# First-layer window attention: scores and weights turned and spread through DRAM by DMA, in place of transposes and spreading matmuls on TensorE

## The chip, the core and the metric

The kernel runs on one core of one Trainium2 chip. The metric is the device time of one execution in microseconds; the median of the runs shown is given. Engines are called PE (TensorE, matmul), DVE (VectorE), ACT (ScalarE), POOL (GpSimd) and SP (SyncE, which here only issues transfers).

## The reference, cut to what matters

The program is four layers, each an attention with a residual and a feed-forward part with a residual, on x of 16 x 64 x 512 values with a context of the same shape, all in 32-bit floats. The change touches only the attention of layer 0, a window attention. Its 64 rows are channels (8 heads of 8), its 512 columns are positions, and each position looks at 16 neighbours:

```python
q = _pointwise(Wq, bq, layernorm(x))        # 64x64 weights, over channels
k = _pointwise(Wk, bk, cond); v = _pointwise(Wv, bv, cond)
k = jnp.pad(k, ((0, 0), (0, 0), (8, 7))); v = jnp.pad(v, ((0, 0), (0, 0), (8, 7)))
idx = jnp.arange(T)[:, None] + jnp.arange(16)[None, :]
dots = jnp.einsum('bhdt,bhdtw->bhtw', qh, k_win) * 8 ** -0.5
attn = softmax(dots, axis=-1)               # over the 16 offsets w
out = jnp.einsum('bhtw,bhdtw->bhdt', attn, v_win)
return _pointwise(Wo, bo, out)
```

After it come an int8-like feed-forward part (layer 0), a grouped attention with normed queries and keys (layer 1), an MXFP4 feed-forward part, and layers 2 and 3.

## The kernel before

**Tiles.** The tokens lie in 8 tiles of 128 rows (two batch entries of 64) by 512 columns. The first layers work on four pairs of tiles.

**Two lanes and the order of TensorE.** Lane a (`main`) runs layer 1's attention, `normed_attention`; lane b (`side`) runs ahead of it through layer 0 (`first_layers`: `WindowAttention`, then `Int8Ffn`), pair by pair. Both are generators that yield a cost in ticks after each step. `merged` draws them together: for each tick of `main` it advances `side` by `rate` ticks, and a `Need` makes it advance `side` until a mark is passed. This order is TensorE's program order (`manual_schedule` for PE alone). The other engines and the SP queue are ordered by a scheduler from expected readiness and this order. While lane b does the first pair, lane a computes its context keys (`context_keys`, L679, rate 1.1). After that, lane a's heads run over one pair (16 units of 11.4 ticks) while lane b prepares the next pairs, at the rates of the list in `main`: 0.88, 0.8, 0.8, 0.72 for the four pairs.

**Window attention on one pair** (`weights`, then `output` for each tile). A tile's 128 rows are 16 heads of 8 channels, so a pair has NH = 32 heads. For each of 4 groups of 4 offsets, DVE multiplies queries by shifted keys into `prod` (L293), and PE sums each head's 8 channels with a 0/1 matrix into a bank whose 128 rows are 4 offsets by 32 heads (L300). ACT copies it to `dots` (L308). A softmax over the offsets needs them along a row, so PE transposes `dots` by quarters of 128 positions (`ps_dotT`, L316); DVE takes maximum, difference and sum (L324, L325, L328), ACT the exponential (L326), POOL the scaling (L330); PE turns the result back (`ps_att`, L137 through `transposed`), and ACT copies it to `att` (L338).

`output` must give each of a tile's 128 channels the weight of its head. For each group of offsets, PE multiplies 32 rows of `att` by a 0/1 matrix `spread` for each of 4 offsets (`ps_exp`, L367); DVE multiplies by the shifted values into `pv` (L377); POOL adds the upper two products to the lower two (L379), then the remaining two into `acc` (L383, or L385 and L386). `project` multiplies `acc` by the output weights on PE (L356). `n_sums` says how many `acc` are projected per tile: 4 for the first pair (one per group), 1 for the others. DVE adds bias and residual (L395).

**Buffers.** `prod` and `pv` share 2 buffers of 4 x 512 values per row; `e` and the context tiles share 3 of 512; lane b has 4 of the 8 PSUM banks.

**Transfers.** All are issued from SP's queue, in order. In this part they are lane a's: weights (L622, 1.5 MB, and L631, 1 MB, each once for two units), saved context keys and values (`s`, L701; loads L714 and L719). Lane b has only the context tiles (L247).

Of the kernel before, what the change touches and what calls it, by code (L numbers as in the profile page):

```python
# [46 lines left out]
PAGE = 2048  # L47

# [149 lines left out]
class WindowAttention:  # L198
# [6 lines left out]
    def __init__(self, es, ln, ctx_in, wt, bias):  # L205
# [7 lines left out]

        self.spread = pool.tile([P, 2 * P], F32, tag="spread", name="spread")
# [7 lines left out]
        for w in range(self.NG):  # L222
            rows = slice(w * NH, (w + 1) * NH)
            nc.vector.tensor_copy(
                self.spread[rows].rearrange("p (h d) -> p h d", d=8),
                bc(k.ident[rows, rows], 2, 8),
            )
# [17 lines left out]
    def context(self, t):  # L245
        cn = self.pool.tile([P, D], F32, tag="row", name="cn", bufs=3)
        self.ln.nc.sync.dma_start(cn, self.ctx_in[t * P : (t + 1) * P, :])  # L247
        return cn
# [23 lines left out]
    def products(self, name):  # L272
        return self.pool.tile([P, self.NG, D], F32, tag="prod", name=name, bufs=2)

    def weights(self, tiles):
# [8 lines left out]
        for xn, cn in zip(xns, cns):  # L284
            self.kept.append(self.inputs(xn, cn))
            yield 3.0
        dots = pool.tile([P, WIN // NG, D], F32, tag="dots", name="dots")
        for g in range(WIN // NG):
# [19 lines left out]
            nc.scalar.copy(dots[:, g, :], ps)  # L308

        self.att = pool.tile([P, WIN // NG, D], F32, tag="att", name="att")  # L310
        es_of = {}
        for c in range(NC + 2):
            if c < NC:
                ps = ln.bank([P, WIN, NH], "ps_dotT")
                for g in range(WIN // NG):
                    nc.tensor.transpose(  # L316
                        ps[:, g * NG : (g + 1) * NG, :].rearrange("p w h -> p (w h)"),
                        dots[:, g, c * P : (c + 1) * P],
                        ln.k.ident,
                    )  # L320
                e = pool.tile([P, D], F32, tag="row", name="e", bufs=3)
                e = e.rearrange("p (w h) -> p w h", w=WIN)
                mx = ln.small.tile([P, NH], F32, tag="mx0", name="mx0")
                nc.vector.tensor_reduce(mx, ps.rearrange("p w h -> p h w"), AX.X, ALU.max)  # L324
                nc.vector.tensor_tensor(e, ps, bc(mx, 1, WIN), ALU.subtract)  # L325
                nc.scalar.activation(e, e, AF.Exp, scale=8.0**-0.5)  # L326
# [5 lines left out]
            if c <= NC:  # L332
                yield 3.0
# [1244 lines left out]
```

## Time and profile before

| | |
|---|---|
| median of three runs | 1778.39 us (1776.37 to 1782.56) |
| profiled execution, its own time | 1772.04 us |
| its span, first to last instruction | 1770.2 us |
| busy: PE, DVE, ACT, POOL | 1686.6, 965.3, 615.3, 501.4 us |
| mean granted clock of PE | 0.991 |
| DMA | 154.23 MB, 25.7% of 16 engines' span on the main queue |
| layer 0 attention | from 8 to 819 us, beside lane a's work |
| lane a's first query matmul | 213.5 us |

A row of the profile's groups gives line, engine, operation, what is written and read, the count, the busy time and the mean of one in ns, and after it the idle time of that engine just before these instructions and what ended it. A 32-bit matmul leaves two records, so "x256" of `ps_exp` are 128 matmuls. A line of the timeline gives start, duration, engine, line, operation and the number of merged records, and in brackets the idle time before it. Waits of the SP queue are given as total, number and longest, in us.

### The profile page before, as it was taken

What the parts mean: (1) busy time and instruction counts of PE and PEld (TensorE: products, weight loads), DVE (VectorE), ACT (ScalarE), POOL (GpSimd) and SP (SyncE); (2) the same over time, 40 slices, a digit from 0 to 9 for tenths busy, and PEclk for the clock granted to TensorE, in tenths of its full rate; (3) what the DMA queues carried; (4) which work ended last, traced back from release to release, by engine and by line L of the source; (5) the groups of instructions that cost most, each with busy time, mean ns of one, the idle gap of its engine ahead of it and who ended that gap; (6) DMA issues with size and microseconds to landing.
All of it is one profiled execution on the core that took longest, in us unless ns stands there. A gap on an engine that the chain in (4) does not pass through costs nothing.

```text
span 1770.2 us, 21537 instructions
## 1 busy us (share of the span) xinstructions
PE 1686.6 (95%) x7592; PEld 960.9 (54%) x7596; DVE 965.3 (55%) x2042; ACT 615.3 (35%) x1933; POOL 501.4 (28%) x494
## 2 busy tenths in 40 slices
PE   7999999999999999999999999999999999999999
PEld 2323455565554665555655656655566655556664
DVE  6644477666665656556587426648425534521335
ACT  2312244334432434424334335521224422223332
POOL 1443225632245431366222213310112201110012
PEclk9989999999999999999999999999999999999999
DMA  9211223213232333222263233031211011111120
GB/s 295 94 66 60 90 79 104 93 66 127 83 128 69 105 105 104 92 105 92 72 238 118 79 106 139 27 116 48 87 43 66 19 45 48 42 66 44 36 66 24
DMA packets 62362, 154.23 MB, mean 87 GB/s; under 512 B 31536, under 2 KB 40624, under 8 KB 50352
## 3 DMA queue, kind: packets, MB, share of 16 engines
q1 hardware_dynamic: 62256, 152.86, 25.7%
q8 instruction: 61, 1.00, 0.2%
q14 instruction: 45, 0.37, 0.1%
HBM read 142.35 MB, written 10.49 MB: 86 GB/s over the span
## 4 chain that ended last, share of the span: by engine, by line
PE 46%; DVE 6%; POOL 3%; ACT 3%; DMA 1%; issue 1%; SPq 0%; ACTq 0%; POOLq 0%; DVEq 0%
PE ps_wo L592 9%; PE ps_q L1291 4%; PE ps_q L722 3%; PE ps_o L1144 3%; PE ps_h L1119 3%; PE ps_a L583 3%; PE ps_s L543 2%; PE ps_v L1238 2%; PE ps_k L1275 2%; PE ps_pT L137 2%; PE ps_kv L740 2%; PE ps_wo L1035 2%; PE ps_q L967 2%; PE ps_o L1206 2%; ACT p L558 1%; PE ps_v L946 1%
## 5 line engine op out<-in xcount | busy, mean ns | idle before, releaser
L592 PE MATMUL ps_wo<-l1a_o,aT 128*128 128x512 f32 x512 | 234.4, 601 | 0.8 <-issue 0.6
L722 PE MATMUL ps_q<-l1a_w,kvT 128*128 128x512 f32 x512 | 230.8, 593 | 0.0
L567 POOL TENSOR_TENSOR p<-p,sm 128x512 f32<-128x512 f32 x96 | 105.9, 1103 | 437.4 <-DVE sm L566 380.5
L558 ACT ACTIVATE p<-ps_s,mx 128x128 f32<-128x128 f32 x384 | 135.5, 367 | 247.6 <-DVE mx L554 210.8
L119 POOL TENSOR_TENSOR r<-r,mhalf 128x5 f32<-128x5 f32 (+1 forms) x96 | 101.9, 1062 | 284.2 <-DVE r L669 279.9
L592 PEld LDWEIGHTS ps_wo<-l1a_o,aT 128*128 128x128 f32 x512 | 95.5, 192 | 121.0 <-issue 120.0
L722 PEld LDWEIGHTS ps_q<-l1a_w,kvT 128*128 128x128 f32 x512 | 92.7, 190 | 96.7 <-issue 96.6
L141 DVE TENSOR_TENSOR x<-x,ps_wo 128x512 f32<-128x512 f32 x104 | 70.6, 679 | 132.8 <-PE ps_wo L592 106.9
L740 PE MATMUL ps_kv<-l1a_w,kvT 128*128 128x256 f32 x512 | 124.2, 386 | 5.0 <-ACT qn L732 2.6
L679 PE MATMUL ps_ckv<-l1a_kv,kvT 128*64 128x512 f32 x512 | 123.2, 625 | 2.3 <-DMA l1a_kv<-in_l1a_kv 2.3
L668 DVE TENSOR_REDUCE r<-sq 128x5 f32<-128x640 f32 (+1 forms) x96 | 65.4, 682 | 108.4 <-ACT sq L748 55.6
L740 PEld LDWEIGHTS ps_kv<-l1a_w,kvT 128*128 128x128 f32 x512 | 93.4, 192 | 20.2 <-ACT qn L732 4.3
L119 POOL TENSOR_TENSOR rs<-rs,mhalf 128x1 f32<-128x1 f32 x64 | 37.1, 583 | 220.0 <-DVE rs L128 213.3
L553 DVE TENSOR_REDUCE mx<-ps_s 128x4 f32<-128x512 f32 x96 | 65.6, 684 | 61.2 <-PE ps_s L543 61.2
L756 DVE TENSOR_TENSOR qn<-qn,r 128x512 f32<-128x512 f32 x64 | 47.6, 743 | 92.3 <-POOL r L119 91.1
L543 PEld LDWEIGHTS ps_s<-kT,qT 128*128 128x128 f32 (+1 forms) x704 | 89.1, 192 | 14.7 <-issue 5.5
L379 POOL TENSOR_TENSOR pv<-pv 128x1024 f32<-128x1024 f32 x32 | 75.2, 2350 | 71.9 <-DVE pv L377 66.5
L543 PE MATMUL ps_s<-kT,qT 128*128 128x128 f32 (+1 forms) x704 | 92.1, 277 | 0.0
L137 PE MATMUL ps_pT<-ident,p 128*128 128x128 f32 x512 | 75.3, 276 | 16.7 <-DVE pT L574 7.0
L293 DVE TENSOR_TENSOR prod<-qs,kp 128x1024 f32<-128x1024 f32 x64 | 80.8, 1294 | 17.9 <-ACT kp L269 14.9
L592 PE MATMUL ps_wo<-l3a_o,aP 128*128 128x512 f32 x192 | 86.5, 598 | 1.4 <-DVE pT L574 0.5
L377 DVE TENSOR_TENSOR pv<-ps_exp,vp 128x512 f32<-128x512 f32 x128 | 80.9, 680 | 9.0 <-PE ps_exp L367 8.9
(202 smaller groups left out, 2878.5 us busy)
## 6 DMA issues: line engine op xcount, KB each, us to landing
l1a_w<-in_l1a_w SPq DMA_DIRECT2D x32, 1536.0 KB, 6.9
l1a_o<-in_l1a_w SPq DMA_DIRECT2D x32, 1024.0 KB, 5.0
s<-ckv SPq DMA_DIRECT2D x32, 256.0 KB, 2.0
l3a_w<-in_l3a_w SPq DMA_DIRECT2D x6, 1024.0 KB, 5.9
l3a_o<-in_l3a_w SPq DMA_DIRECT2D x8, 768.0 KB, 4.3
l1a_kv<-in_l1a_kv SPq DMA_DIRECT2D x4, 1024.0 KB, 6.1
kT<-s SPq DMA_DIRECT2D x64, 64.0 KB, 2.6
v<-s SPq DMA_DIRECT2D x128, 32.0 KB, 2.3
```

What stands on the lines that cost most here:

```text
L119: self.nc.gpsimd.tensor_tensor(out, v, self.k.mhalf[:, : v.shape[1]], ALU.pow)
L137: self.nc.tensor.transpose(ps[:, c, :], src[:, c * P : (c + 1) * P], ident)
L293: nc.vector.tensor_tensor(prod[:, w : w + 2, :], bc(qs, 1, 2), windows(kp, g * NG + w, 2, D), ALU.mult,)
L377: nc.vector.tensor_tensor(pv[:, w, :], ps, vp[:, o : o + D], ALU.mult)
L379: nc.gpsimd.tensor_tensor(pv[:, 0:2, :], pv[:, 0:2, :], pv[:, 2:4, :], ALU.add)
L543: nc.tensor.matmul(ps[:, i, :], lhsT=qT[:, i // 2, 2 * (i % 2) : 2 * (i % 2) + 2, :].rearrange("p g s -> p (g s)"), rhs=kTs[i // 2], start ...
L558: nc.scalar.activation(p[:, i, :], ps[:, i, :], AF.Exp, bias=mx[:, i : i + 1], scale=self.scale, accum_out=sm[:, i : i + 1],)
L567: nc.gpsimd.tensor_tensor(p, p, bc(sm, 2, P), ALU.mult)
L592: self.nc.tensor.matmul(ps, lhsT=a, rhs=wo[:, g, :], start=g == 0, stop=g == len(chunks) - 1)
L679: nc.tensor.matmul(ps[j * S : (j + 1) * S], lhsT=k.context(c, 2 * t + 1 - j), rhs=w_pair[hp][:, c, :], start=c == 0, stop=c == NC - 1,)
L722: nc.tensor.matmul(ps, lhsT=k.stream(c, t), rhs=w_qkv[n][0][:, c, :], start=c == 0, stop=c == NC - 1,)
L740: nc.tensor.matmul(ps, lhsT=k.stream(c, t), rhs=w_qkv[n][1][:, c, :], start=c == 0, stop=c == NC - 1,)
```

## The change

The transposes, the spreading matmuls and their copies go. Each group of `dots` is stored to a DRAM tile as soon as it is copied; two loads bring the scores back with head and quarter of the positions on the 128 rows and the 16 offsets along a row. The softmax runs there in place, in four parts of 32 positions. One store puts the weights in DRAM by group of offsets and head, and one load for each group and tile (`load_spread`) brings 16 heads back, each repeated on 8 rows. DVE multiplies two offsets at a time, in place. `prod` and `pv` have 3 buffers, the row tiles 2. Of the first pair's values, POOL still adds the upper two products to the lower two, and the two left are both projected on PE, so there are 8 projections per tile. The rates of `main` become 0.9, 0.85, 0.85, 0.72, and some yields change.

```diff
@@ -45,6 +45,15 @@
 
 
 PAGE = 2048
+
+
+def offsets(ap, first, n):
+
+    return bass.AP(
+        tensor=ap.tensor,
+        offset=ap.offset + first,
+        ap=[list(ap.ap[0]), [P, 4], [1, n], [1, P]],
+    )
 
 
 class Block:
@@ -210,8 +219,6 @@
 
         self.group = pool.tile([P, 2, NH], F32, tag="group", name="group")
         nc.gpsimd.memset(self.group, 0.0)
-
-        self.spread = pool.tile([P, 2 * P], F32, tag="spread", name="spread")
         for i in range(2):
             nc.vector.tensor_reduce(
                 self.group[:, i, 16 * i : 16 * (i + 1)],
@@ -219,12 +226,9 @@
                 AX.X,
                 ALU.add,
             )
-        for w in range(self.NG):
-            rows = slice(w * NH, (w + 1) * NH)
-            nc.vector.tensor_copy(
-                self.spread[rows].rearrange("p (h d) -> p h d", d=8),
-                bc(k.ident[rows, rows], 2, 8),
-            )
+        self.dram = es.enter_context(
+            ln.tc.tile_pool(name="turned", bufs=2, space=bass.MemoryType.DRAM)
+        )
 
         self.wbd = pool.tile([P, 4, P], F32, tag="wbd", name="wbd")
         nc.gpsimd.memset(self.wbd, 0.0)
@@ -243,7 +247,7 @@
                 yield from self.output(i, t, n_sums)
 
     def context(self, t):
-        cn = self.pool.tile([P, D], F32, tag="row", name="cn", bufs=3)
+        cn = self.pool.tile([P, D], F32, tag="row", name="cn", bufs=2)
         self.ln.nc.sync.dma_start(cn, self.ctx_in[t * P : (t + 1) * P, :])
         return cn
 
@@ -270,7 +274,7 @@
         return qs, kp, vp
 
     def products(self, name):
-        return self.pool.tile([P, self.NG, D], F32, tag="prod", name=name, bufs=2)
+        return self.pool.tile([P, self.NG, D], F32, tag="prod", name=name, bufs=3)
 
     def weights(self, tiles):
 
...
+        NQ = P // NH
+        dram = self.dram.tile([WIN, NH, D], F32, tag="dots", name="dots_d")
         dots = pool.tile([P, WIN // NG, D], F32, tag="dots", name="dots")
+        att = dots.rearrange("p g (w n) -> p (g w) n", n=P)
         for g in range(WIN // NG):
             ps = ln.bank([P, D], "ps_dot")
             for i, (qs, kp, _) in enumerate(self.kept):
@@ -306,42 +315,48 @@
                     )
                 yield 3.0
             nc.scalar.copy(dots[:, g, :], ps)
-
-        self.att = pool.tile([P, WIN // NG, D], F32, tag="att", name="att")
-        es_of = {}
-        for c in range(NC + 2):
-            if c < NC:
-                ps = ln.bank([P, WIN, NH], "ps_dotT")
-                for g in range(WIN // NG):
-                    nc.tensor.transpose(
-                        ps[:, g * NG : (g + 1) * NG, :].rearrange("p w h -> p (w h)"),
-                        dots[:, g, c * P : (c + 1) * P],
-                        ln.k.ident,
-                    )
-                e = pool.tile([P, D], F32, tag="row", name="e", bufs=3)
-                e = e.rearrange("p (w h) -> p w h", w=WIN)
-                mx = ln.small.tile([P, NH], F32, tag="mx0", name="mx0")
-                nc.vector.tensor_reduce(mx, ps.rearrange("p w h -> p h w"), AX.X, ALU.max)
-                nc.vector.tensor_tensor(e, ps, bc(mx, 1, WIN), ALU.subtract)
-                nc.scalar.activation(e, e, AF.Exp, scale=8.0**-0.5)
-                sm = ln.small.tile([P, NH], F32, tag="sm0", name="sm0")
-                nc.vector.tensor_reduce(sm, e.rearrange("p w h -> p h w"), AX.X, ALU.add)
-                nc.vector.reciprocal(sm, sm)
-                nc.gpsimd.tensor_tensor(e, e, bc(sm, 1, WIN), ALU.mult)
-                es_of[c] = e
-            if c <= NC:
-                yield 3.0
-            if c >= 2:
-                ps = ln.transposed(
-                    es_of[c - 2].rearrange("p w h -> p (w h)"), WIN // NG, "ps_att"
-                )
-                nc.scalar.copy(self.att[:, :, (c - 2) * P : (c - 1) * P], ps)
-                yield 0.5
+            nc.sync.dma_start(
+                dram[g * NG : (g + 1) * NG].rearrange("w h n -> (w h) n"), dots[:, g, :]
+            )
+        for part in (slice(0, WIN - NG), slice(WIN - NG, WIN)):
+            nc.sync.dma_start(
+                att[:, part, :], dram[part].rearrange("w h (q n) -> (h q) w n", q=NQ)
+            )
+        yield 4.0
+        for c in range(NQ):
+            e = att[:, :, c * NH : (c + 1) * NH]
+            mx = ln.small.tile([P, NH], F32, tag="mx0", name="mx0")
+            nc.vector.tensor_reduce(mx, e.rearrange("p w n -> p n w"), AX.X, ALU.max)
+            nc.vector.tensor_tensor(e, e, bc(mx, 1, WIN), ALU.subtract)
+            nc.scalar.activation(e, e, AF.Exp, scale=8.0**-0.5)
+            sm = ln.small.tile([P, NH], F32, tag="sm0", name="sm0")
+            nc.vector.tensor_reduce(sm, e.rearrange("p w n -> p n w"), AX.X, ALU.add)
+            nc.vector.reciprocal(sm, sm)
+            nc.gpsimd.tensor_tensor(e, e, bc(sm, 1, WIN), ALU.mult)
+            yield 3.0
+
+        self.att = self.dram.tile([WIN // NG, NH, NG * D], F32, tag="att", name="att_d")
+        nc.sync.dma_start(self.att.rearrange("g h (q n) -> (h q) g n", q=NQ), dots)
+        self.spread = []
+        for _ in range(2):
+            self.load_spread()
+        yield 8.0
+
+    def load_spread(self):
+
+        n = len(self.spread)
+        if n == 2 * self.WIN // self.NG:
+            return
+        i, g = divmod(n, self.WIN // self.NG)
+        pv = self.products("pv").rearrange("p w n -> p (w n)")
+        heads = slice(i * self.NH // 2, (i + 1) * self.NH // 2)
+        self.ln.nc.sync.dma_start(pv, bc(self.att[g, heads, :], 1, 8))
+        self.spread.append(pv.rearrange("p (q w n) -> p q w n", w=self.NG, n=P))
 
     def output(self, i, t, n_sums):
 
         ln, nc = self.ln, self.ln.nc
-        NH, NG = self.NH, self.NG
+        NG = self.NG
         n_groups = self.WIN // NG
         vp = self.kept[i][2]
 
@@ -354,43 +369,46 @@
             if first:
                 po = ln.bank([P, D], "ps_o")
             nc.tensor.matmul(
-                po, lhsT=self.wbd[:, 3, :], rhs=sums.pop(0), start=first, stop=last
+                po.rearrange("p (q n) -> p q n", n=P),
+                lhsT=self.wbd[:, 3, :],
+                rhs=sums.pop(0),
+                start=first,
+                stop=last,
             )
 
         acc = None
         for g in range(n_groups):
-            pv = self.products("pv")
-            pss = []
-            for w in range(NG):
-                rows = slice(w * NH, (w + 1) * NH)
-                ps = ln.bank([P, D], "ps_exp")
-                nc.tensor.matmul(
-                    ps,
-                    lhsT=self.spread[rows, i * P : (i + 1) * P],
-                    rhs=self.att[rows, g, :],
-                    start=True,
-                    stop=True,
-                )
-                pss.append(ps)
-            for w, ps in enumerate(pss):
-                o = g * NG + w
-                nc.vector.tensor_tensor(pv[:, w, :], ps, vp[:, o : o + D], ALU.mult)
+            pv = self.spread[i * n_groups + g]
+            for w in range(0, NG, 2):
+                two = pv[:, :, w : w + 2, :]
+                nc.vector.tensor_tensor(two, two, offsets(vp, g * NG + w, 2), ALU.mult)
+            if len(sums) == 2:
+                project(False)
+                project(False)
+            self.load_spread()
             yield 2.0
-            nc.gpsimd.tensor_tensor(pv[:, 0:2, :], pv[:, 0:2, :], pv[:, 2:4, :], ALU.add)
+            nc.gpsimd.tensor_tensor(
+                pv[:, :, 0:2, :], pv[:, :, 0:2, :], pv[:, :, 2:4, :], ALU.add
+            )
             yield 1.4
+            if n_sums == 2 * n_groups:
+                sums += [pv[:, :, 0, :], pv[:, :, 1, :]]
+                continue
             if g % (n_groups // n_sums) == 0:
                 acc = self.pool.tile([P, D], F32, tag="acc", name="acc", bufs=2)
-                nc.gpsimd.tensor_tensor(acc, pv[:, 0, :], pv[:, 1, :], ALU.add)
+                acc = acc.rearrange("p (q n) -> p q n", n=P)
+                nc.gpsimd.tensor_tensor(acc, pv[:, :, 0, :], pv[:, :, 1, :], ALU.add)
             else:
-                nc.gpsimd.tensor_tensor(acc, acc, pv[:, 0, :], ALU.add)
-                nc.gpsimd.tensor_tensor(acc, acc, pv[:, 1, :], ALU.add)
+                nc.gpsimd.tensor_tensor(acc, acc, pv[:, :, 0, :], ALU.add)
+                nc.gpsimd.tensor_tensor(acc, acc, pv[:, :, 1, :], ALU.add)
             yield 1.4
             if sums:
                 project(False)
             if (g + 1) % (n_groups // n_sums) == 0:
                 sums.append(acc)
-        yield 6.0
-        project(True)
+        yield 6.0 if len(sums) == 1 else 3.0
+        while sums:
+            project(len(sums) == 1)
         x = ln.k.x[t]
         nc.vector.scalar_tensor_tensor(x, po, self.bcol[:, 3:4], x, ALU.add, ALU.add)
 
@@ -1444,7 +1462,7 @@
                 i["l0f_down"],
                 [i[f"l0f_{n}"] for n in ("ig", "iu", "sg", "su", "ii", "sd")],
             )
-            first = attention.run(groups[0], 4)
+            first = attention.run(groups[0], 8)
             yield next(first)
             for c in range(NC):
                 for r in range(2):
@@ -1477,7 +1495,7 @@
     def main():
         yield Need(0, 1.1)
         yield from normed_attention(
-            a, groups, [0.88, 0.8, 0.8, 0.72], i["l1a_w"], i["l1a_kv"], i["l1a_n"]
+            a, groups, [0.9, 0.85, 0.85, 0.72], i["l1a_w"], i["l1a_kv"], i["l1a_n"]
         )
         yield Need(len(groups) + 1, 1.0)
         a.pages(ctx)
```

## The prediction

> **What bounds the kernel now.** I read the head of the page, then the groups of TensorE (PE), then the timelines around the first layer, then the queue of SyncE (SP).
>
> ```profile
> span 1770.2 us, 21537 instructions
> PE 1686.6 (95%) x7592; PEld 960.9 (54%) x7596; DVE 965.3 (55%) x2042; ACT 615.3 (35%) x1933; POOL 501.4 (28%) x494
> ...
> L367 PE MATMUL ps_exp<-att,spread 32*128 32x512 f32 x256 | 48.3, 645 | 12.8 <-DVE pv L377 5.7 <-ACT att L338 4.2 <-DVE x L395 2.8
> ...
> L356 PE MATMUL ps_o<-acc,wbd 128*128 128x512 f32 x28 | 15.1, 622 | 0.0
> ...
> L316 PE MATMUL ps_dotT<-ident,dots 128*128 128x128 f32 x64 | 9.7, 274 | 0.0
> ...
> L137 PE MATMUL ps_att<-ident,e 128*128 128x128 f32 x64 | 9.4, 275 | 0.0
> ```
>
> TensorE is busy 1686.6 of 1770.2 us and idle only 83.6. Nothing else passes 55%. So a microsecond of TensorE work taken away is a microsecond won, as long as TensorE, whose order is written out, finds its next operand ready. The rows of L367, L316 and L137 are what the change takes away. The row of L356 shows that today the projections of the first layer never wait (0.0): their sums are always early.
>
> ```profile
> 82.50 1.13 PE L367 MATMUL ps_exp<-att,spread 32*128 32x512 f32 x6
> 85.11 1.52 PE L367 MATMUL ps_exp<-att,spread 32*128 32x512 f32 x2 [1.47 <-DVE pv L377]
> 86.56 0.69 PE L137 MATMUL ps_ckT<-ident,ckn 128*128 128x128 f32 x2
> ```
>
> This is TensorE's timeline in the first pair: the fourth spreading matmul waits for a bank that VectorE frees. After it the granted clock is 0.57 from 85 to 90 us, and the next group of context keys takes 6.29 us, its neighbours 3.65. Two more such groups (5.58, 5.35) follow later waits.
>
> ```profile
> 277.80 1.27 POOL L330 TENSOR_TENSOR e<-e,sm 128x512 f32<-128x512 f32 x1
> 277.87 1.75 DVE L756 TENSOR_TENSOR qn<-qn,r 128x512 f32<-128x512 f32 x1 [0.43 <-POOL r L119]
> 289.08 0.69 DVE L756 TENSOR_TENSOR qn<-qn,r 128x512 f32<-128x512 f32 x1 [1.28 <-POOL r L119]
> ```
>
> VectorE (DVE) and GpSimd (POOL) here exclude each other: a product of two SBUF tiles that starts 0.07 us after a GpSimd add takes 1.75 us; alone it takes 0.69.
>
> ```profile
> SPq L622 <- PE ps_kv L740: 319.2, 29, 16.3
> SPq L631 <- PE ps_wo L592: 203.6, 27, 26.8
> SPq L719 <- PE ps_a L583: 199.3, 54, 12.9
> ```
>
> The waits of the SP queue: its head mostly stands before a load of the main lane (weights L622, L631, values L719) until TensorE frees the buffer. All new transfers join this one queue.
>
> **What the Trainium skill says.** (1) "SBUF — State Buffer", section "Who interferes with whom": a VectorE instruction with two SBUF inputs and a GpSimd instruction that reads SBUF lock each other out. The 1.75 us above agrees. (2) "TensorE: Matmul & The Clock Gate", section "Part 3: Packing small matmuls — row/col tiling": matmuls of 32 rows in different row groups run together, 3.07 times as fast for four. The trace agrees: four of L367 take 1.14 us when nothing holds them, against 4 x 0.92 for full ones (L592, 234.4/256). So the spreading costs 48.3 us and not 118. (3) The same page, Part 1: idle time lowers the granted clock; the 0.57 agrees. (4) "DMA: Bandwidth & Descriptors", section "Why a DMA increments its semaphore by 16 and not by 1": a transfer is spread over as many of 16 engines as divide both outermost sizes. All new ones have 128 (the broadcast source 16), so all get 16; no run here shows these shapes yet.
>
> **The change part by part.** Sums are against the profiled execution (1772.0 us, span 1770.2); the median of the runs shown is 1778.4, 6.4 above it, and I carry the difference over.
>
> *Taken from TensorE.* 128 spreading matmuls: 48.3 us and 12.8 of idle time before them, 61.1. 128 transposes: 9.7 + 9.4 = 19.1. The three groups at the low clock: 2.6 + 1.9 + 1.7 = 6.3. *Added:* the first pair makes 16 projections for 8, 8 x 0.92 = 7.3. Together 61.1 + 19.1 + 6.3 - 7.3 = **79 us** off TensorE.
>
> *Hidden, priced at nothing.* ScalarE loses 16 copies of 0.6 us. GpSimd loses the 8 adds of L383 in the first pair (10 us), but keeps the 2.35 us add of every group: TensorE sums only the last two of four products. VectorE's products go from 128 x 0.68 = 87 to 64 x 1.22 (the row of L293, same shape, two SBUF operands) = 78 us. Its maxima now read SBUF with a stride; the strided sum L328 takes 1.05 us where the maximum from PSUM takes 0.68, so 16 x 0.37 = 6 us more. VectorE is at about 62% in this part. Added DMA is 4 x (1 + 1 + 1 + 8) = 44 MB to the 154 MB that use 26% of the engines, 44 issues of 0.35 us on SP. All these lie beside TensorE's work; what they cost is delay, next.
>
> *The new chain.* Scores go to DRAM, return turned, are weighted, go to DRAM again and return spread. TensorE meets the result at the first projection. For pairs 2 to 4, from the end T0 of the last dot matmul: copy 0.6, store of 256 KB 2.0 (row of s), load of 256 KB 2.8 (row of cn), issue 1: 6.4. Four softmax quarters of 1.05 + 0.69 + 1.05 + 0.35 = 3.14 us VectorE: 12.6, while the main lane takes 4.35 us of VectorE per unit of 11.7 us (L668, L669, L756, L757, L574, L553, L554, L566, L141 in VectorE's timeline): 12.6/0.63 = 20. GpSimd 1.3. Store and load of 1 MB, 5.0 each (row of l1a_o): T0 + 38. Then eight groups. Before, the product read PSUM and could run beside GpSimd; now it shares the lock, so the times add: 2.44 + 2.35 + 1.27 for the first group of a tile, 2.44 + 2.35 + 2.54 for the others, 28 per tile, 56 per pair; with about 20% of the lock taken by L756, L567 and L119, 70. The last sum is ready at **T0 + 108**.
>
> *Where TensorE stands then.* Its order is set by the yields. From T0 to the last projection there were 3 + 17 + 2 x 25.2 = 70.4 side ticks, and there will be 3 + 24 + 2 x 25.2 = 77.4. Before, this took 98.4, 115.2 and 110.3 us (pairs 2 to 4), 14.9 of them side work, so 1.19, 1.42 and 1.36 us per tick at rates 0.88, 0.8, 0.8. At 0.9, 0.85, 0.85 and with one projection of 1 us: T0 + 91, T0 + 104, T0 + 100. So TensorE waits 17, 4 and 8 us, and 2 us each time for the low clock: **35 us**. The projection heads TensorE's queue, so all the main lane's matmuls stand behind it.
>
> *First pair.* T0 is 42.9. Same steps, with the main lane at 24% of VectorE: store and load until 50, softmax until 68, 1 MB out and back 77.5, product 80, add 82.5. TensorE comes to the projection 30.4 ticks after T0; a context unit is 3.96 us per 3.7 ticks at rate 1.1, 0.97 us per tick: 72.5. Wait 10, low clock 2: **12 us**. After that a group needs (2.44 + 2.35)/0.84 = 5.7 us of the lock against 3.4 ticks and two projections, 5.1 us; about even. Two loads ahead on three buffers leave each 1 MB load two periods, over 10 us for 5.
>
> *Sum:* 79 - 35 - 12 = 32 us. 1772 - 32 = 1740; on the runs 1778.4 - 32 = **1746 us**.
>
> *Bounds of what the trace doesn't show.* Chain: if the main lane yields the lock and VectorE (softmax 14, groups 56), T0 + 88, no wait in pairs 2 to 4. If the queue orders fit badly, T0 + 128. I take 108 because the lock is seen and the durations are rows of this trace. GpSimd's adds on strided halves: 2.35 us (same size) up to a quarter more, 20 us of GpSimd in all and inside that span. Short 512-byte pieces in the turned load: 2.8 to 6 us.
>
> **Rivals.** (A) The above, chance 0.47. (B) The chain keeps up, as the projections did before (idle 0.0) and as VectorE's order, which is not written out, lets the softmax run together: only the first pair waits. 79 - 10 = 69 us, 1709; chance 0.27. Against it: the lock. (C) Slower: the SP queue. The stores and loads of the chain stand behind a load of the main lane that waits for TensorE; the mean wait for L622 is 319.2/29 = 11 us, for L631 7.5. Two of the four hops hit by 8.5 us put the end at T0 + 125: waits 34 + 21 + 25, clock 6, first pair 12, together 98 against 79: 19 us slower, 1797. It decides from T0 + 119. For it: the head of that queue is nearly always blocked. Against it: the queue is ordered by expected readiness, and the loads of s, issued the same way, hold TensorE up nowhere. Chance 0.18. (D) Between: one hop hit, waits eat the gain, about 1775; 0.08.
>
> **Numbers.** A and B are faster, with a small part of A in the band; D is mostly within 0.3%, about what a measurement of this kernel can tell from no change; C is slower. Faster 0.76, same 0.07, slower 0.17. The range takes B's better end and most of C: 1702 to 1792; A's own is 1722 to 1768.
>
> **What would show it.** TensorE's busy time falls by about 73 us or a little less (67.4 + 6.3 - 7.3, plus new slow matmuls), with no rows of ps_exp, ps_dotT and ps_att. The projection L356 gets idle time before it, released by GpSimd: about 40 us for A, under 12 for B, over 80 for C. Products of 1.22 us stretched to 2 and more, and GpSimd adds likewise, show the lock; their absence is B. The page's DMA total rises to about 198 MB. Wrong altogether would be idle time before the main lane's own matmuls: loads late behind the new transfers.

## The result and the profile after

| | before | after |
|---|---|---|
| median | 1779.05 us (4 runs) | 1808.82 us (4 runs, 1807.66 to 1813.10) |
| ratio | | 1.0171, 95% interval 1.0145 to 1.0196 |
| profiled execution, span | 1770.2 us | 1808.0 us |
| TensorE busy, idle | 1686.6, 83.6 us | 1660.0, 148.0 us |
| mean granted clock of TensorE | 0.991 | 0.965 |

The kernel is 30 us slower; the prediction said 32 us faster, and its range ended at 1792. TensorE has 27 us less work and 64 us more idle time. The head of the page after:

```profile
span 1808.0 us, 20870 instructions
PE 1660.0 (92%) x7228; PEld 960.2 (53%) x7228; DVE 989.4 (55%) x1974; ACT 605.1 (33%) x1917; POOL 524.3 (29%) x486
```

Where the idle time lies is in TensorE's waits of the kernel after. The columns are what waits, for what, the total in us, how often, and the longest:

```profile
PE ps_qT L146 <- DVE qn L774: 21.0, 7, 4.6
PE ps_kv L758 <- ACT p L576: 16.2, 3, 6.6
PE ps_kT L146 <- ACT p L576: 15.1, 7, 3.5
PE ps_pT L146 <- DVE x L150: 14.0, 7, 6.1
PE ps_ckT L146 <- DVE ckn L711: 11.0, 3, 4.8
...
PE ps_o L371 <- POOL pv L390: 7.1, 2, 6.5
```

The projection of the sums (L371), where the prediction put 40 us, waits 7.1. The five lines above it are waits of the **main lane** (layer 1's attention), whose own steps the diff doesn't touch. Two are for an operand: normed queries `qn` and context keys `ckn`. The other three name softmax weights `p` and residual `x`, but `ps_kv` and `ps_kT` don't read `p`, and `ps_pT` doesn't read `x`. By the kernel's text the main lane uses four PSUM banks in turn, ScalarE frees the bank of the scores by computing `p` from it, and VectorE frees that of `ps_wo` by adding it to `x`; so these three are most likely waits for a bank. Before, the transposes of `qn` had no idle time at all. Line numbers moved by 9 (helpers) to 18: L774 was L756, L128 was L119.

Who makes VectorE and ScalarE late shows in VectorE's and GpSimd's groups. Before, the products (L377) took 0.68 us for 512 values a row and read PSUM:

```profile
L377 DVE TENSOR_TENSOR pv<-ps_exp,vp 128x512 f32<-128x512 f32 x128 | 80.9, 680 | 9.0 <-PE ps_exp L367 8.9
L379 POOL TENSOR_TENSOR pv<-pv 128x1024 f32<-128x1024 f32 x32 | 75.2, 2350 | 71.9 <-DVE pv L377 66.5
L756 DVE TENSOR_TENSOR qn<-qn,r 128x512 f32<-128x512 f32 x64 | 47.6, 743 | 92.3 <-POOL r L119 91.1
```

After:

```profile
L384 DVE TENSOR_TENSOR pv<-pv,vp 128x1024 f32<-128x1024 f32 x64 | 103.7, 1641 | 31.1 <-DMA pv<-att_d 31.1
L390 POOL TENSOR_TENSOR pv<-pv 128x1024 f32<-128x1024 f32 x32 | 83.0, 2594 | 76.7 <-DVE pv L384 45.9 <-DVE r L687 20.0 <-DVE mx L572 5.1
L774 DVE TENSOR_TENSOR qn<-qn,r 128x512 f32<-128x512 f32 x64 | 53.4, 834 | 100.1 <-POOL r L128 98.9 <-POOL kp L266 1.1
```

Two things are to be seen. The products average 1641 ns, against 1220 where nothing disturbs them (the median; the longest takes 3377), and GpSimd's adds 2594 against 2350. And VectorE stood 31.1 us before products whose spread load had not landed. The spread loads' size and median time from issue to landing, beside a weight load of the same 1 MB:

```profile
pv<-att_d SPq DMA_DIRECT2D x32, 1024.0 KB, 9.6
l1a_o<-in_l1a_w SPq DMA_DIRECT2D x32, 1024.0 KB, 5.1
```

A landing time includes what a load stands behind an earlier one, and it runs from 6.7 to 18.6 us here; single packets are compared below. How the pieces meet is in the timelines of VectorE, GpSimd and TensorE after, in the last pair (start, duration, instruction, and in brackets the idle time before it):

```profile
761.75 2.36 DVE L384 TENSOR_TENSOR pv<-pv,vp 128x1024 f32<-128x1024 f32 x2 [3.72 <-DMA pv<-att_d]
764.03 0.17 DVE L687 TENSOR_SCALAR r<-r 128x5 f32<-128x5 f32 x1
...
768.68 1.75 DVE L774 TENSOR_TENSOR qn<-qn,r 128x512 f32<-128x512 f32 x1 [1.06 <-POOL r L128]
...
772.28 2.97 DVE L384 TENSOR_TENSOR pv<-pv,vp 128x1024 f32<-128x1024 f32 x1
775.18 1.22 DVE L572 TENSOR_SCALAR mx<-mx 128x4 f32<-128x4 f32 x1
```
```profile
764.19 2.34 POOL L390 TENSOR_TENSOR pv<-pv 128x1024 f32<-128x1024 f32 x1 [10.81 <-DVE r L687]
766.50 2.15 POOL L128 TENSOR_TENSOR r<-r,mhalf 128x5 f32<-128x5 f32 x1
```
```profile
754.97 1.89 PE L758 MATMUL ps_kv<-l1a_w,kvT 128*128 128x256 f32 x8
...
770.49 1.11 PE L146 MATMUL ps_qT<-ident,qn 128*128 128x128 f32 x4 [4.56 <-DVE qn L774]
771.39 0.42 PE L146 MATMUL ps_kT<-ident,kn 128*128 128x128 f32 x1
778.05 3.78 PE L758 MATMUL ps_kv<-l1a_w,kvT 128*128 128x256 f32 x8 [6.24 <-ACT p L576]
```

VectorE stands 3.72 us before the products for a load. Behind them in its queue is L687, 0.17 us of the main lane's norm. GpSimd's part of that norm (L128, 5 values a row) then stands behind an add of 2.34 us and takes 2.15 us itself, where it took 1.17 at 747 us; `qn` takes 1.75 us in place of 0.69. TensorE waits 4.56 us for it. The last step of the next softmax maximum (L572) stands behind a product stretched to 2.97 us, ScalarE can compute `p` only then, and TensorE waits 6.24 us. Its next group takes 3.78 us where the same group took 1.89 at 755 us: the granted clock is 0.50 from 778 to 782 us and was 1.00 at 755.

### The profile page after: what moved, and what is told of

The parts are those of the page before. It is cut to its first block, busy times and chain, and to the rows that moved or that the text cites. A ratio compares the mean times of both kernels' runs of the same rounds, so it can differ in the third digit from the quotient of the medians.

```text
span 1808.0 us, 20870 instructions
## 1 busy us (share of the span) xinstructions
PE 1660.0 (92%) x7228; PEld 960.2 (53%) x7228; DVE 989.4 (55%) x1974; ACT 605.1 (33%) x1917; POOL 524.3 (29%) x486
## 2 busy tenths in 40 slices
DMA packets 79704, 200.33 MB, mean 111 GB/s; under 512 B 32496, under 2 KB 49776, under 8 KB 63600
## 4 chain that ended last, share of the span: by engine, by line
PE 66%; DVE 13%; POOL 10%; DMA 5%; ACT 3%; issue 2%; SPq 1%; POOLq 0%; ACTq 0%; DVEq 0%
PE ps_wo L610 12%; PE ps_q L740 7%; PE ps_q L1309 5%; PE ps_kv L758 4%; DMA pv<-att_d 4%; PE ps_ckv L697 4%; PE ps_a L601 3%; PE ps_s L561 3%; PE ps_o L1162 3%; PE ps_h L1137 3%; POOL pv L390 3%; PE ps_v L1256 2%; PE ps_k L1293 2%; PE ps_pT L146 2%; POOL r L128 2%
## 5 line engine op out<-in xcount | busy, mean ns | idle before, releaser
L585 POOL TENSOR_TENSOR p<-p,sm 128x512 f32<-128x512 f32 x96 | 112.9, 1177 | 420.1 <-DVE sm L584 322.6
L128 POOL TENSOR_TENSOR r<-r,mhalf 128x5 f32<-128x5 f32 (+1 forms) x96 | 105.9, 1103 | 326.2 <-DVE r L687 323.0
L758 PE MATMUL ps_kv<-l1a_w,kvT 128*128 128x256 f32 x512 | 136.7, 415 | 19.8 <-ACT p L576 16.2
L758 PEld LDWEIGHTS ps_kv<-l1a_w,kvT 128*128 128x128 f32 x512 | 101.4, 208 | 39.3 <-ACT p L576 17.3
L128 POOL TENSOR_TENSOR rs<-rs,mhalf 128x1 f32<-128x1 f32 x64 | 38.8, 613 | 282.6 <-DVE rs L137 274.6
L384 DVE TENSOR_TENSOR pv<-pv,vp 128x1024 f32<-128x1024 f32 x64 | 103.7, 1641 | 31.1 <-DMA pv<-att_d 31.1
L774 DVE TENSOR_TENSOR qn<-qn,r 128x512 f32<-128x512 f32 x64 | 53.4, 834 | 100.1 <-POOL r L128 98.9
L390 POOL TENSOR_TENSOR pv<-pv 128x1024 f32<-128x1024 f32 x32 | 83.0, 2594 | 76.7 <-DVE pv L384 45.9
L146 PE MATMUL ps_pT<-ident,p 128*128 128x128 f32 x512 | 79.1, 287 | 23.7 <-DVE x L150 14.0
L146 PEld LDWEIGHTS ps_pT<-ident,p 128*128 128x128 f32 x512 | 63.9, 148 | 49.9 <-issue 40.1
```

Of the source, the lines that this page charges most:

```text
L128: self.nc.gpsimd.tensor_tensor(out, v, self.k.mhalf[:, : v.shape[1]], ALU.pow)
L146: self.nc.tensor.transpose(ps[:, c, :], src[:, c * P : (c + 1) * P], ident)
L384: nc.vector.tensor_tensor(two, two, offsets(vp, g * NG + w, 2), ALU.mult)
L390: nc.gpsimd.tensor_tensor(pv[:, :, 0:2, :], pv[:, :, 0:2, :], pv[:, :, 2:4, :], ALU.add)
L585: nc.gpsimd.tensor_tensor(p, p, bc(sm, 2, P), ALU.mult)
L758: nc.tensor.matmul(ps, lhsT=k.stream(c, t), rhs=w_qkv[n][1][:, c, :], start=c == 0, stop=c == NC - 1,)
```

## Experiments

Four theories. **Slow loads** (theory 1): VectorE's queue stands still for late spread loads, with the main lane behind. **Lock** (theory 2): VectorE's products, with two SBUF operands now, and GpSimd's adds exclude each other, and stretch all that stands behind them. **GpSimd's queue**: the lane's small work stands behind adds that wait for products. **Chain** (theory 3): the turned path, or SP's queue that carries it, is too long. Ratios are to the kernel before on the same chip, 1772.5 to 1774.4 us; a version is called faster or slower where the interval of its ratio leaves out 1.

### The lock and the queue

**e2_memset** replaces GpSimd's adds by memsets of the same destinations, so sums are not computed.

```diff
-            nc.gpsimd.tensor_tensor(pv[:, :, 0:2, :], pv[:, :, 0:2, :], pv[:, :, 2:4, :], ALU.add)
+            nc.gpsimd.memset(pv[:, :, 0:2, :], 0.01)
...
-                nc.gpsimd.tensor_tensor(acc, acc, pv[:, :, 0, :], ALU.add)
+                nc.gpsimd.memset(acc, 0.01)
```

> The kernel after, but GpSimd's adds of the products are replaced by memsets of the same destinations, so the products are not summed. The memsets only write, so they should not exclude VectorE's products with two SBUF inputs; they still sit in GpSimd's queue at the same places. Theory 2 (lock): the products fall from 1641 to about 1220 ns, the main lane's waits behind them go, and the time falls by 25 us or more, to under 1784. Theory 1 (slow loads): the products get shorter but VectorE still waits about 30 us for the loads; the time falls by less than 12 us.

Measured: 1751.74 us, **0.9875** (0.9846 to 0.9904), so 53 us are gone, and products take 1220 ns each. But a memset of 1024 values takes 0.95 us against 2.35 for the add, and those of `acc` no longer depend on the products, so GpSimd's queue got shorter too. **e4_long** takes that out of the comparison: two or three memsets for an add, nearly all on `pv`, so that they wait for the products as the adds did.

> GpSimd's adds of the spread products (L390, L400, L402, L403) are replaced by memsets of the same buffers of about the same length (2.43 us in place of a group's add, 1.05 to 1.6 us in place of the others), which depend on the products as the adds did; so the sums are not computed. The shared lock of VectorE and GpSimd is then hardly taken by them, while GpSimd's queue stays as full. Theory 'lock': products of L384 come down to about 1.22 us and the time falls nearly as far as with the short memsets, 1750 to 1765 (ratio 0.99 to 0.996). Theory 'queue' (what hurts is that small GpSimd work of the main lane, L128, stands behind 2.4 us adds that wait for late products): the time stays near the changed kernel's, 1790 to 1805 (ratio 1.01 to 1.018), although the products take 1.22 us. In between, both carry a part.

Measured: 1760.56 us, **0.991** (0.9876 to 0.9944). The group of products in this kernel:

```profile
L384 DVE TENSOR_TENSOR pv<-pv,vp 128x1024 f32<-128x1024 f32 x64 | 76.6, 1220 | 55.4 <-DMA pv<-att_d 53.3 <-POOL pv L391 2.1
```

GpSimd is busy 494.9 us, nearly the 524.3 of after, VectorE waits for loads longer than before (53.3 us), and still 46 of the 53 us are gone ((1.0171 - 0.991) x 1775). So what the adds cost is the lock, not GpSimd's occupancy. One reservation: VectorE's and GpSimd's orders are made by the scheduler and shifted a little with the edit; TensorE's is the same in the two traces, instruction for instruction.

**e6_dveadd** moves these adds to VectorE.

```diff
-            nc.gpsimd.tensor_tensor(
+            nc.vector.tensor_tensor(
                 pv[:, :, 0:2, :], pv[:, :, 0:2, :], pv[:, :, 2:4, :], ALU.add
             )
```

> The changed kernel with the adds of L390, L400, L402 and L403 on VectorE in place of GpSimd; same results, VectorE busy some 75 us more, GpSimd some 115 us less. Theory 'lock and GpSimd queue': products at 1.22 us, the small GpSimd work of the main lane no longer behind adds, idle time of TensorE before its norm and softmax operands falls; 1755 to 1785 (ratio 0.99 to 1.007). Theory 'VectorE's in-order queue is what holds the main lane': the adds make that queue longer, and TensorE waits for qn and p as much as or more than in the changed kernel; 1800 to 1830.

Measured: 1758.15 us, **0.9889** (0.9845 to 0.9933). This version is faster than both kernels. The head of its page and two groups of VectorE:

```profile
PE 1641.9 (94%) x7228; PEld 945.3 (54%) x7228; DVE 1005.0 (57%) x2048; ACT 606.4 (35%) x1917; POOL 374.5 (21%) x412
...
L384 DVE TENSOR_TENSOR pv<-pv,vp 128x1024 f32<-128x1024 f32 x64 | 78.4, 1244 | 35.2 <-DMA pv<-att_d 35.2
```
```profile
L390 DVE TENSOR_TENSOR pv<-pv 128x1024 f32<-128x1024 f32 x32 | 39.2, 1224 | 0.2
```

With 74 instructions more, VectorE is busy only 16 us longer, since products and `qn` shrink; the add takes 1.22 us there in place of 2.35 to 2.59 on GpSimd, and TensorE's wait for `qn` falls from 21.0 to 6.1 us. A longer queue on VectorE was not the trouble.

**e18_lock_before** puts the lock into the kernel before. The spreading matmuls run, but the products read `att` itself, so the spreading is left out of the result.

```diff
-            for w, ps in enumerate(pss):
-                o = g * NG + w
-                nc.vector.tensor_tensor(pv[:, w, :], ps, vp[:, o : o + D], ALU.mult)
+            for w in (0, 2):
+                two, v2 = bc(self.att[:, g, :], 1, 2), windows(vp, g * NG + w, 2, D)
+                nc.vector.tensor_tensor(pv[:, w : w + 2, :], two, v2, ALU.mult)
```

> The kernel before, with one edit: the products of the spread weights read the weights' own SBUF tile (of 128 rows, as 64 instructions of two SBUF inputs) in place of the PSUM banks of the spreading matmuls, which are still computed, so the values are wrong. Nothing else moves: no new transfer, same matmuls. VectorE's products and GpSimd's adds now lock each other out. Theory 'lock': products stretch from 1.22 to 1.5 us and more, adds beyond 2.35, TensorE waits for the operands of its main lane, and the time rises by 15 to 45 us, 1790 to 1820 (ratio 1.008 to 1.025), although VectorE has less to do and TensorE no longer waits for banks. Rival 'the lock alone is hidden, it needs the late loads in VectorE's queue': 1760 to 1780 (ratio 0.993 to 1.004).

Measured: 1859.84 us, **1.0491** (1.0455 to 1.0528), 87 us where 15 to 45 were expected, without one new transfer. Its group of products, then TensorE's waits:

```profile
L377 DVE TENSOR_TENSOR pv<-att,vp 128x1024 f32<-128x1024 f32 x64 | 132.5, 2106 | 27.1 <-POOL acc L386 15.8 <-POOL acc L383 8.2 <-ACT att L338 3.1
```
```profile
PE ps_s L543 <- DVE x L141: 24.3, 2, 15.3
PE ps_pT L137 <- DVE x L141: 20.0, 6, 14.9
PE ps_qT L137 <- DVE qn L756: 19.8, 4, 10.6
```

The products need 2.1 us and stand at the head of VectorE's queue until GpSimd frees one of only two buffers; the main lane waits up to 15 us. TensorE waits for `qn` and `x` again, as after. The products no longer depend on the spreading matmuls either, and the scheduler moved part of VectorE's work. So the 87 us are the price of the lock together with these buffers and that order, and not a part of the change's sum. But the lock needs no late load to do harm.

### The loads

**e1_distinct** lets a load read 128 different rows in place of 16 rows eight times, so the values meet weights of other heads and offsets; the order of TensorE, VectorE and GpSimd stays the same, instruction for instruction.

```diff
-        self.ln.nc.sync.dma_start(pv, bc(self.att[g, heads, :], 1, 8))
+        self.ln.nc.sync.dma_start(pv, self.att.rearrange("g h x -> (g h) x"))
```

> The kernel after, but each spread load reads 128 different rows of the DRAM tile of weights (all 4 groups of offsets by 32 heads) instead of 16 rows repeated 8 times; the weights that meet the values are thus the wrong ones. Same bytes, same piece of 8 KB per row, same issue, same dependence on the store, same order on every engine. Theory 1 (the repeated rows are read at half speed, the loads land late, and the products that wait for them hold the head of VectorE's queue, with the main lane's work behind): a load lands in 5 to 7 us for 9.6, VectorE's wait for these loads falls from 31 to under 10 us, and the time by 25 to 50 us, to 1760-1784. Theory 2 (the lock between VectorE and GpSimd sets the pace): the time stays within 10 us of 1809. Theory 3 (the SP queue issues the loads late): within 10 us as well, the waits of the loads on SP unchanged.

Measured: 1794.91 us, 1.0119 (1.0084 to 1.0154).

```profile
L384 DVE TENSOR_TENSOR pv<-pv,vp 128x1024 f32<-128x1024 f32 x64 | 111.3, 1762 | 5.5 <-DMA pv<-att_d 5.4
```

Landing falls from 9.6 to 5.7 us and VectorE's wait for loads from 31.1 to 5.4, yet only some 9 us come back, and the intervals of this run and of after overlap. The products now take 1762 ns; that they meet more adds because they start earlier is a reading, not tested. Alone, theory 1 falls.

**e12_both** joins this edit with e2's memsets, **e17_dve_distinct** with e6's adds on VectorE.

> Both edits together: 128 different rows in each spread load, and memsets for GpSimd's adds (wrong weights, products not summed). If the two causes are independent, the gains add. If both are needed and nothing else stalls TensorE, the time comes to TensorE's work alone: 1779 less about 67 us of spreading and transposes plus 7 of added projections, less part of the old waits, about 1715. If a third cause (SP queue, latency of the chain) is large, it stays above 1745.

> The kernel with the adds on VectorE; a spread load reads 128 different rows once each in place of 16 rows eight times, so the weights are wrong and only the time is of use. It bounds what the repeats cost here: if 31 us as with memsets, 1725 to 1735 (ratio 0.973 to 0.978); if VectorE's longer queue is the limit instead, 1745 to 1758.

Measured: 1720.21 us, **0.9696** (0.9665 to 0.9727), and 1732.50 us, **0.9765** (0.9737 to 0.9794). Without the lock, the repeats cost 32 us with memsets (0.9875 - 0.9696) and 22 us with the adds on VectorE (0.9889 - 0.9765). Both causes are real, and the second shows clearly only once the first is gone. With both gone, 1720 us is close to the 1715 expected of TensorE's work alone, so theory 3 isn't needed for the loss.

Why are loads with repeats slow? **e5_pad** stores the weights with a row pitch of 12 KB in place of 8, by four stores in place of one; **e11_dve_split** (on e6) makes eight DMAs of a load, one for each copy; **e14_two_copies** and **e15_four_copies** (on e6) store two or four copies, so that a row is read four times or twice.

```diff
+        for d in range(8):
+            self.ln.nc.sync.dma_start(pv[d::8], self.att[g, heads, :])    # e11
...
+        for c, q in ((c, q) for c in range(2) for q in range(NQ)):       # e14
+            nc.sync.dma_start(
+                self.att[:, :, c, q * D : (q + 1) * D].rearrange("g h n -> h g n"),
+                dots[q::NQ],
+            )
```

> The changed kernel with the DRAM copy of the weights laid out with a row pitch of 12 KB in place of 8 KB; it is stored by four DMAs, one for each quarter, in place of one. The loads still read each of 16 rows eight times. If the slow loads come from the pitch, the spread loads fall from 9.6 us to about 5.5 and the time to about 1795 to 1800 (as with distinct rows, ratio 1.012); if they come from reading the same rows eight times, they stay at 9 to 10 us and the time at 1800 to 1810.

> The kernel with the adds on VectorE; each spread load split into eight DMAs, one for each of the eight copies, each of which reads 16 different rows of 8 KB and writes every eighth partition. Same bytes, same results; SP issues 256 DMAs in place of 32. If the loads are slow because several DMA engines read one row at the same time, a load's packets come down to about 0.31 us and the load to about 5 to 6 us, and the time falls to 1725 to 1745 (ratio 0.973 to 0.985), as distinct rows were worth 31 us once the lock was gone. If it is the number of times a row is read in all, the loads stay at 9 to 12 us and the time at 1755 to 1765; if SP's 224 more issues delay the main lane's loads, 1765 or more.

> The kernel with the adds on VectorE (0.989), with the weights stored twice in DRAM (8 stores of 128 KB for each pair in place of one of 1 MB), so that a spread load reads 32 rows four times each in place of 16 rows eight times. If loads are slow by the number of engines that read one row at once, the mean packet of 8 KB falls from 0.59 us towards 0.45 us, and the time to 1740 to 1755 (ratio 0.98 to 0.988); if the repeats don't matter, it stays at 1755 to 1765.

> The same with four copies (16 stores for each pair), 64 rows read twice each. By the same theory packets near 0.35 to 0.4 us and 1725 to 1750 (ratio 0.972 to 0.985), less what the stores cost: 16 issues of about 0.6 us on SP lengthen the chain by some 9 us per pair, and if TensorE waits for that, 1755 to 1770.

The mean time of a spread load's packet of 8 KB is worked out from the packet records of each trace: all packets of that size, less those of the kernel before:

| | packet, us | time, us | ratio (interval) |
|---|---|---|---|
| after | 0.59 | 1808.82 | 1.0171 (1.0145 to 1.0196) |
| e5_pad | 0.55 | 1802.08 | 1.0148 (1.0106 to 1.0190) |
| e6_dveadd | 0.59 | 1758.15 | 0.9889 (0.9845 to 0.9933) |
| e11_dve_split | 0.44 | 1859.24 | 1.0477 (1.0452 to 1.0502) |
| e14_two_copies | 0.33 | 1779.99 | 1.0034 (1.0022 to 1.0047) |
| e15_four_copies | 0.32 | 1781.47 | 1.0032 (1.0014 to 1.0051) |
| e17_dve_distinct | 0.34 | 1732.50 | 0.9765 (0.9737 to 0.9794) |

The pitch hardly matters. Rows read eight times are slow, rows read four times are as fast as distinct ones. The number of different rows grows as the repeats fall, so the two aren't told apart, and why the step lies between four and eight stays open. None of these cures paid: e5 can't be told from after, and e11, e14 and e15 are slower than e6. In these three the trouble looks like the one that rival C had named, the issuing queue. In e11 SP spends 256 x 0.587 us on issues, and TensorE waits 102 us at the projection. In e14 the sums come late too, as TensorE's waits and SP's timeline there show:

```profile
PE ps_o L375 <- DVE acc L407: 50.6, 3, 19.9
```
```profile
495.00 5.92 SPq L340 DMA_DIRECT2D att_d<-dots  x8
501.03 1.19 SPq L741 DMA_DIRECT2D v<-s  x2
511.78 0.35 SPq L644 DMA_DIRECT2D l1a_w<-in_l1a_w  x1
512.67 2.00 SPq L357 DMA_DIRECT2D pv<-att_d  x3
```

The last softmax step of VectorE ends at 493.6. The eight stores (256 KB each by the page, not the 128 expected) take 5.92 us of SP, and the loads stand until 512.67 behind a weight load (L644). **e19_act_stores** issues the eight stores from ScalarE's queue.

> The kernel with adds on VectorE and two copies of the weights, with its eight stores for each pair issued from ScalarE's queue in place of SP's. If SP's queue (stores and loads behind weight loads of the main lane that wait for TensorE) makes the 57 us of waits for the last sums, these fall to under 15 us and the time to 1728 to 1745 (ratio 0.974 to 0.984); if the loads alone, still on SP, are what stands there, or ScalarE's queue holds the stores as long, 1765 to 1780.

Measured: 1763.45 us, **0.9921** (0.9886 to 0.9956). The 57 us of waiting for sums become 5, so SP's queue was their cause in e14; e15 was not tested so. The time beats before but not e6, and the expected 1728 to 1745 was missed. TensorE now waits 8.7 and 9.7 us for ScalarE's copies `aT` and `kT`, and ScalarE's queue in this run shows why:

```profile
719.77 10.40 ACTq L340 DMA_DIRECT2D att_d<-dots  x8
730.22 0.28 ACT L770 ACTIVATE sq<-ps_kv 128x128 f32<-128x128 f32 x1 [13.06 <-DMA att_d<-dots]
```

Here ScalarE issues the eight stores for 10.40 us, its next step of the main lane (L770) stands behind them, and TensorE waits 6.66 us for `aT`; in pair 2 it waits 6.74 us for `kT` in the same way. The harm moved to another queue that both lanes share.

### One part alone

**e3_turn** only turns scores and weights through DRAM and loads the weights back for the spreading matmuls, with the change's rates and softmax yields; **e7_sums_alone** only sums the first pair on TensorE in the kernel before; **e8_after_sums4** and **e9_dve_sums4** undo that in after and in e6, and **e13_dve_split_sums4** in e11.

```diff
-            first = attention.run(groups[0], 8)
+            first = attention.run(groups[0], 4)      # e8, e9; e7 the other way round
```

> One part of the change alone: scores are turned and weights turned back through DRAM (store 1 MB, load 1 MB, store 1 MB, load 1 MB per pair), but the weights are spread on TensorE as before and summed on GpSimd as before; rates and yields of the softmax part as in the changed kernel. It removes the 19 us of transposes from TensorE and keeps the spreading, and has neither the 8 MB of spread loads per pair nor products with two SBUF inputs. Theories 1 and 2: no long stalls, 1760 to 1772. Theory 3 or a chain that is too long by itself: the spreading matmuls, which come earlier in TensorE's order than the projections, wait for the turned weights, and the time is above 1779.

> The kernel before with one part of the change alone: the first pair's eight sums go to TensorE (8 projections for the first pair in place of 2), scores and weights as before. By the prediction's own price this adds 8 times about 0.9 us of TensorE, some 7 us, and takes 12 us of waiting for the first pair's sums away: 1765 to 1780 (ratio 0.997 to 1.004). A rival, that the part is itself the loss because sums come later than the matmul queue can wait for, gives 1790 or more.

> The changed kernel with one part undone: the first pair's values summed on GpSimd into four tiles as before (4 projections), scores and weights turned and spread by DMA. The part alone had cost the kernel before 1.15% (22 us). Theory 'the part itself costs' (7 to 10 us of TensorE work and an order of the lanes that fits the matmul queue worse): about the same 15 to 22 us come back here, 1785 to 1793 (ratio 1.005 to 1.01). Rival 'only the order of that kernel was unlucky, the part is worth its projections alone': 5 to 10 us come back, 1798 to 1804.

> As the kernel with the adds on VectorE (0.989), with the first pair summed into four tiles as before. If the first pair's part costs 15 us or more whatever stands around it: 1735 to 1743 (ratio 0.978 to 0.982). If its cost is that of 16 more matmul instructions of 0.59 us alone: 1746 to 1752. If the adds that the part takes away matter more here, since VectorE does them: no gain, 1755 to 1765.

> The last two edits together: adds on VectorE, loads split in eight, first pair summed into four tiles. If both pay and add up: 1715 to 1735 (ratio 0.967 to 0.978). If one of them gives nothing: 1735 to 1750.

Measured: e3 1793.55 us, 1.0119 (1.0085 to 1.0153); e7 1796.30 us, 1.0115 (1.0071 to 1.0159); e8 1807.64 us, 1.0191 (1.0170 to 1.0211); e9 1759.76 us, 0.9927 (0.9906 to 0.9948); e13 1868.15 us, 1.0544 (1.0518 to 1.0569). In e3 the products read PSUM and stay at 680 ns, and TensorE waits for the loads of the weights (12.0 us, three times): the turned chain is too late for the spreading matmuls, which stood sooner in the order than the projections do. That is about half of e3's 22.5 us of added idle time. In e7 (16 projections of the first pair in place of 8, not the 8 in place of 2 of its expectation) TensorE has 7.1 us more work and 12.5 us more idle time, spread over many waits of the whole run; the projections of the first pair wait only 1.7 us, so it isn't the late sums that the rival named, and which shift in the lanes makes it was not settled. In after, in e6 and in e11 the same part costs nothing: undoing it gains nothing, outside both ranges expected of e8 and as the last of the three of e9. So e7's loss isn't a part of the change's loss, and single parts of a change to the lanes' order don't add up.

## Why the prediction was wrong

**The step that failed** is in the part on VectorE and GpSimd: "All these lie beside TensorE's work; what they cost is delay, next." The delay was then priced at one place only, the projection. VectorE and GpSimd carry the main lane's norms and softmax in the same queues, and L687 and L128 above stood there behind a product and an add. So a product that waits for a load, and a product and an add that exclude each other, delay the main lane's operands and the freeing of its PSUM banks, and TensorE stops there. The prediction saw the lock (1.75 us for `qn`), added its times on the side lane ("2.44 + 2.35"), and did not ask what stands behind it on the main lane. With the lock taken away, e4 and e6 came to 0.991 and 0.989, which is 46 and 50 of the 62 us between the predicted 1746 and the measured 1808.8.

**The loads were mis-sized:** 5.0 us each from the row of `l1a_o`, measured 9.6. That is worth 22 to 32 us without the lock and some 9 with it. The number of engines, which the prediction took from the Trainium skill's "DMA: Bandwidth & Descriptors" (section "Why a DMA increments its semaphore by 16 and not by 1"), fits the trace: the 128 packets of 8 KB that follow the first spread load's issue take 0.57 us each in the mean and 4.99 us together, so about 15 were under way at once. What no run had shown was the repeats.

**The chain** was nearly in time: TensorE waited 7.1 us at the projection and not 40. This was rival B's picture for the chain, with the loss elsewhere. **Rival C** had the sign, but by luck: its place was the projection behind SP's queue, which shows as the main wait only in e11, e14 and e15. The prediction also counted 44 added issues on SP; the page after has 60 (16 stores and 8 loads of scores, 4 stores and 32 loads of weights). Its sum doesn't use that number.

**TensorE's busy time** fell by 26.6 and not by 73. The rows of L367, L316 and L137 did go, less the added projections, 60 us. The other 33 go with the clock, 0.965 for 0.991: by an estimate from these figures, a factor of 1.027 on 1627 us is up to 44. So the waits were in part paid twice, as at 778 us above; no run separates the two. The row `ps_kv<-l1a_w,kvT` went from 386 to 415 ns in the mean.

**What held:** the DMA total (200.33 MB for 198), single products stretched to 2 us and more as the sign of the lock, and the last sentence's guess that it would be wrong if the main lane's own matmuls waited, though for VectorE's and GpSimd's work and not for their loads. The size of the gain was there to be had: with neither lock nor repeats, e17 reached 0.9765, 42 us below before, where 32 had been predicted. It reads the weights of other heads, so it is a bound and not a usable version; the best usable one is e6, 20 us below.

## What to carry to other kernels

Price an edit on an engine that two lanes share by what stands behind it in that engine's queue, not by the lane it belongs to: list, for each new wait or stretched instruction, the next small instruction of the other lane and who waits for it. When an operand moves from PSUM to SBUF, look for the adds that the other of VectorE and GpSimd runs beside it; here moving them to VectorE paid 50 us ((1.0171 - 0.9889) x 1775), though VectorE was the busier. Then look at the issuing queue before adding transfers to mend another one.

## What the runs showed of the hardware

The lock between a VectorE instruction with two SBUF inputs and a GpSimd instruction that reads SBUF is stated in the Trainium skill's "SBUF — State Buffer", section "Who interferes with whom". The runs agree, and they give its size here: products 1.22 us alone, 1.64 to 1.76 in the mean beside GpSimd's adds (after, e1), 2.11 in e18; adds of 512 values (L385) 1.79 in e18 against 1.27 us before. The skill's "Perfetto Trace Analysis", section "Optimizing Scalar/DVE Operations", warns that moving work between VectorE and GpSimd might not help; here moving it toward VectorE did, and a memset on GpSimd, which reads nothing, left the products at 1.22 us.

A load that reads 16 rows of 8 KB eight times took 0.59 us per packet; with the same rows in two copies, four times each, 0.33. The row pitch (8 or 12 KB) changed it by 0.04.
